# Rotary table and key norm column as one array, loaded inside the branch on the score bound (Perceiver layer, one core)

## The chip, the cores and the metric

The kernel runs on one core of one Trainium2 chip. The metric is the device time of one execution in microseconds, and a kernel's figure is the median of its runs. Profiles are of one execution each. In what follows PE is TensorE's matmul, PEld its weight loads, DVE is VectorE, ACT is ScalarE, POOL is GpSimd, and SP is the sync engine, which only asks for transfers here; "ACTq" and "SPq" are the queues from which ScalarE and SP ask for DMAs. L104 is line 104 of the kernel before.

## The reference

One layer over 256 tokens of width 512, in three residual parts: cross attention, a state-space (Mamba-2) block, and a mixture of 32 experts with 6 per token and one shared expert. Only the first part touches the change:

```python
q = rms_norm((x @ wq).reshape(B, L, 16, 128), q_norm_w)
k = rms_norm((x @ wk).reshape(B, L, 4, 128), k_norm_w)
v = (x @ wv).reshape(B, L, 4, 128)
k_ctx = rms_norm((h_ctx_kv @ wk_ctx).reshape(B, T, 4, 128), k_norm_w)     # T = 4096
v_ctx = (h_ctx_kv @ wv_ctx).reshape(B, T, 4, 128)
cos, sin = rope_cache(L, 128, 10000.0, x.dtype)
q = q * cos + rotate_half(q) * sin
k = k * cos + rotate_half(k) * sin
k_full = concatenate([k_ctx, k]); v_full = concatenate([v_ctx, v])        # repeated for 4 heads each
out = softmax(q @ k_full * scale + mask) @ v_full @ wo                    # the 256 own keys are causal
...
x = x + xattn(layernorm(x), ctx); x = x + mamba(layernorm(x)); x = x + moe(layernorm(x))
```

All of it is fp32. `x` is normalised before it is projected, so the queries and own keys need the layer norm, while the 4096 context keys and values need only `ctx_2048`, `wk_ctx` and `wv_ctx`.

## The kernel before, in words

The program has a short common part and then a branch. The common part (L78 to L138) loads the two norm weights into one row, `nw` (L87), and computes from them a bound on the attention scores (L107 to L110). Every engine loads the resulting flag (L1599) and goes into one of two arms, each of which is a full layer; with these inputs it is the arm `layer(lctx, True)`, `bounded`, which subtracts a constant in the softmax instead of a running maximum. Ahead of the flag SP also asks for what the first matmuls need, in this order:

- the first context slice, `ctx0[:, 0]`, 256 KB (L97, recorded as L94);
- the context key weights, the `wkc` half of the tile `wkv`, in three pieces of 256, 256 and 512 KB (L98 to L100, recorded as L95);
- `x_sb`, the tokens, 512 KB (L101);
- the second slice of `ctx0`, 256 KB, and the last two, 512 KB (L102, L103);
- the context value weights `wvc`, 1024 KB (L104).

ScalarE asks for `nw`, and then for three tables: `rope` (cosine and sine of 256 positions by 64 frequencies, 128 KB, L133), `w_bc` (the two norm weights broadcast to all 128 partitions, 128 KB, L135), and `kw_col` (the key norm weight as a column, one word per partition, L138).

Inside the arm SP goes on with the projection weights: `wk`, `wq0`, `wv`, `wq1` to `wq3` of 1024 KB each (`wpiece`, L189), then the next pieces of the context (`load_ctx`, L240). The matmuls of the start run in this order on TensorE: three key pieces of the first context block (`key_piece`, tile `ps_k`, four products over k with one of the four `wkc` slices each; in fp32 a product shows as two rows), eight transposes of the normalised `x` (`turn_xn`, tile `lnT`), the first value piece (`ps_v`, which needs `wvc`), and the self blocks (`ps_self`, with `wk` and `wq`), between which the other pieces of the first context block stand. After that come the attention over nine blocks of keys and values, the state-space part and the experts.

The tables are used by VectorE and ScalarE. `rope_table` (L436) multiplies the cosines and sines by the norm weights, in eight operations, L441 and L442, into a part of `oacc`; `norm_rope` (L446) uses the result when the first self block is done. `bounded_attention` takes two maxima over `w_bc` (L555, L556). `kw_col` scales the queries at L630. On VectorE the layer norm (`bn_stats` L201, then L203, L195, and `xn` at L206) stands in the same in-order queue as L441 and L442. In the program of before, the order there is: both `bn_stats`, one `bn_aggr`, L441, and then the operations of the two groups in turn.

The framework writes each engine's order from its own estimates of the times, except where the code pins it (`keep_in_program_order`, `issue_after`). It also gives the completion of DMAs from SP and ScalarE to eight semaphores in turn: a DMA first waits for the one that had the same semaphore before it, eight places earlier in the common order of both queues. In the program of before, that order begins: `nw`, `ctx0` slice 0, `rope`, `wkc` piece 0, `w_bc`, `kw_col`, `wkc` piece 1, `wkc` piece 2, `x_sb`, `ctx0` slice 1, `ctx0` slices 2 and 3, `wvc`, and, in the arm, `wk`, `wq0`, `wv`, `wq1`. So slice 1 of `ctx0` waits for slice 0, slices 2 and 3 for `rope`, `wvc` for `wkc` piece 0, `wk` for `w_bc`, and `wq0` for `kw_col`.

Of the kernel before, what the change touches and what calls it, by code (L numbers as in the profile page):

```python
# [11 lines left out]
FP = mybir.dt.float32  # L12
# [7 lines left out]
P = 128  # L20
L = 256
NT = L // P
# [9 lines left out]
HALF = HD // 2  # L32
# [34 lines left out]
def rope_tables():  # L67
    inv = (1.0 / np.float32(THETA) ** (np.arange(0, HD, 2, dtype=np.float32) / np.float32(HD))).astype(np.float32)
    freqs = np.outer(np.arange(L, dtype=np.float32), inv).astype(np.float32)
    return np.stack([np.cos(freqs), np.sin(freqs)], axis=1).astype(np.float32)  # L70
# [3 lines left out]
def perceiver_layer(ctx: ExitStack, tc: tile.TileContext, a: dict, out: bass.AP):  # L74
    nc = tc.nc
    V, S, G, TE = nc.vector, nc.scalar, nc.gpsimd, nc.tensor

    early = ctx.enter_context(tc.tile_pool(name="early", bufs=1))  # L78
    const = ctx.enter_context(tc.tile_pool(name="const", bufs=1))
# [49 lines left out]
    blocks_d = [tc.dram_tile((REP, HD, P), FP, name=f"qd{i}") for i in range(NT * NH // REP)]  # L129
    sums_d = [tc.dram_tile((SH, P), FP, name=f"sums{t}") for t in range(NT)]  # L130

    rope = const.tile([P, NT, 2, HALF], FP, name="rope")
    S.dma_start(rope, a["rope"].rearrange("(t p) c h -> p t c h", p=P))  # L133
    w_bc = const.tile([P, 2, HD], FP, name="w_bc")
    S.dma_start(w_bc, a["norm_ws"].partition_broadcast(P))  # L135
    qw_bc, kw_bc = w_bc[:, 0, :], w_bc[:, 1, :]
    kw_col = const.tile([P, 1], FP, name="kw_col")
    S.dma_start(kw_col, a["norm_ws"][1, :].unsqueeze(1))  # L138

    def layer(ctx, bounded):  # L140
        small = ctx.enter_context(tc.tile_pool(name="small", bufs=4))
        wpool = ctx.enter_context(tc.tile_pool(name="wpool", bufs=6))
        kvp = ctx.enter_context(tc.tile_pool(name="kvp", bufs=2))
# [1456 lines left out]
    with tc.If(flag == 1) as arms:  # L1600
        with ExitStack() as lctx:
            layer(lctx, True)
    with arms.Else():
        with ExitStack() as lctx:
            layer(lctx, False)


def expert_weights(wg, wu, wd):

    c = np.ascontiguousarray  # L1610
    gu = np.concatenate([wg, wu], axis=2).reshape(NE, KD, P, 2 * FE).transpose(0, 2, 1, 3).reshape(NE, P, WGU)
    return {"experts": c(np.concatenate([gu, wd[:, 0:P]], axis=2)), "down_rest": c(wd[:, P:])}


def host_layout(i):

    c = np.ascontiguousarray
    f = {k: np.asarray(v) for k, v in i.items()}
    xa, ma, fa = "L0_xattn_", "L0_attn_", "L0_ffn_"
    d = {  # L1620
        "x": c(f["x"][0]),
        "ctxT": c(f["ctx_2048"][0].reshape(NC, CK // P, P, KD, P).transpose(0, 4, 1, 3, 2)),
        "rope": rope_tables(),
        "W_inT": c(f[ma + "W_in"].T),
        "W_outT": c(f[ma + "W_out"].T),
        "by_channel": c(np.concatenate([f[ma + "conv_w"].reshape(XCT, P, CONV).transpose(1, 0, 2).reshape(P, XCT * CONV),
                                        f[ma + "conv_b"].reshape(XCT, P).T, f[ma + "norm_weight"].reshape(DIT, P).T],
                                       axis=1)),
        "by_head": c(np.stack([f[ma + k] for k in ("dt_bias", "A_log", "D")])),
        "sgu": c(np.stack([f[fa + "sg"], f[fa + "su"]], axis=1)),  # L1630
        **expert_weights(f[fa + "wg"], f[fa + "wu"], f[fa + "wd"]),
    }
    d.update({k: c(f[xa + k]) for k in ("wq", "wk", "wv", "wo", "wk_ctx", "wv_ctx")})
    d["norm_ws"] = c(np.stack([f[xa + "q_norm_w"], f[xa + "k_norm_w"]]))
    d.update({k: c(f[fa + k]) for k in ("gate_w", "sd")})
    return d
# [15 lines left out]
```

## Time and profile before

| | |
|---|---|
| median of 3 runs | 985.41 us (983.65 to 986.29) |
| profiled execution, own time | 989.13 us |
| its span, first to last instruction | 987.4 us |
| instructions | 8877 |
| PE busy | 964.3 us (98%) |
| DVE, ACT, POOL busy | 496.5, 388.1, 205.0 us |
| moved by DMA | 125.65 MB, mean 127 GB/s |
| ScalarE's HWDGE queue (q10) | 4178 packets, 5.85 MB |
| SP's queue (q1) | 119216 packets, 77.96 MB |

A timeline row gives start, length, engine, line, operation, and in brackets how long the engine had been idle before and what ended that. A row with "x3" merges three instructions. A row of the waits gives who waited for what, the sum in us, how often, and the longest. A row of the windows gives the stretch, the busy time of PE, PEld, DVE, ACT and POOL in it with the number of instructions, the granted TensorE clock, the busy share of the DMA engines, and GB/s. The ends of matmul rows are modelled, so that TensorE's own pace is better seen from the starts of its weight loads.

### The profile page before, as it was taken

Reading aid. Unit: us, or ns where it says so; the run is one execution under the profiler, and the core shown is the slowest. Engines: PE = TensorE matmul, PEld = TensorE weight load, DVE = VectorE, ACT = ScalarE, POOL = GpSimd, SP = SyncE. Lnnn points to the kernel's source line nnn. Section 1 sums busy time; section 2 is a strip of 40 time slices with the busy share of each in tenths; the row PEclk is TensorE's granted clock in tenths of the full one; section 3 lists DMA queues with packets and bytes.
Section 4 is the critical chain, followed back from the end, with each engine's and each line's share of the span. In section 5 each row is a group of like instructions: output and inputs, shape, how many; then the busy total and the mean of one; then the engine's idle time right before and its main releaser. Section 6 shows DMA issues by size and latency. Waiting matters only on the chain.

```text
span 987.4 us, 8877 instructions
## 1 busy us (share of the span) xinstructions
PE 964.3 (98%) x2730; PEld 453.8 (46%) x2730; DVE 496.5 (50%) x1000; ACT 388.1 (39%) x854; POOL 205.0 (21%) x212
## 2 busy tenths in 40 slices
PE   7999999999999999999999999999999999999995
PEld 3444444444444444444444444444465655455442
DVE  3456554454454544544545445458587666521133
ACT  3645443443444434434434344344153731122220
POOL 4443001101100200200200110000013234545442
PEclk9999999999999999999999999999999999999999
DMA  9733232213304304304113121250046452899973
GB/s 317 237 74 98 76 95 91 71 32 117 85 11 139 85 1 149 75 11 150 53 33 97 67 51 32 72 152 1 0 150 206 171 188 111 319 342 352 381 292 107
DMA packets 131436, 125.65 MB, mean 127 GB/s; under 512 B 80209, under 2 KB 99570, under 8 KB 126130
## 3 DMA queue, kind: packets, MB, share of 16 engines
q1 hardware_dynamic: 119216, 77.96, 26.1%
q0 software_dynamic: 7984, 41.16, 11.4%
q10 hardware_dynamic: 4178, 5.85, 1.6%
q8 instruction: 24, 0.39, 0.2%
q14 instruction: 34, 0.28, 0.1%
HBM read 89.02 MB, written 35.93 MB: 127 GB/s over the span
## 4 chain that ended last, share of the span: by engine, by line
PE 94%; DVE 2%; ACT 1%; POOL 1%; issue 1%; DMA 1%; SPq 0%; DVEq 0%; ACTq 0%
PE oT L592 23%; PE scT L567 23%; PE ps_kv L364 17%; PE ps_egu L218 5%; PE ps_self L218 3%; PE ps_v L218 2%; PE ps_o L790 2%; PE ps_egu L1388 2%; PE ps_k L218 2%; PE ps_ye L1458 2%; PE ps_xbc L218 1%; PE ps_out L984 1%; PE ps_sgu L218 1%; PE xgTp L1369 1%; PE ps_ye L1461 1%; PE ps_yd L924 1%
## 5 line engine op out<-in xcount | busy, mean ns | idle before, releaser
L583 DVE TENSOR_TENSOR lacc<-lacc,prT 128x512 f32<-128x512 f32 x256 | 182.8, 715 | 238.9 <-ACT prT L573 238.2
L573 ACT ACTIVATE prT<-scT,bq,rk 128x512 f32<-128x512 f32 x256 | 198.9, 777 | 253.8 <-PE scT L567 241.7
L567 PE MATMUL scT<-qT,kT 128*128 128x512 f32 x536 | 271.6, 592 | 0.0
L592 PE MATMUL oT<-prT,v 128*128 128x512 f32 x528 | 268.3, 592 | 0.0
L567 PEld LDWEIGHTS scT<-qT,kT 128*128 128x128 f32 x536 | 101.1, 190 | 124.7 <-issue 122.4
L592 PEld LDWEIGHTS oT<-prT,v 128*128 128x128 f32 x528 | 100.2, 190 | 125.8 <-issue 115.5
L196 POOL TENSOR_TENSOR rk<-pv,mhalf 128x4 f32<-128x4 f32 x32 | 32.3, 1010 | 369.2 <-DVE pv L195 369.2
L364 PE MATMUL ps_kv<-wkv,fast 128*128 128x512 f32 x112 | 53.4, 592 | 0.0
L254 ACT ACTIVATE sq<-kraw 128x128 f32<-128x128 f32 x128 | 35.6, 278 | 45.3 <-DVE kraw L382 43.2
L364 PE MATMUL ps_kv<-wkv,ctx 128*128 128x512 f32 x112 | 52.8, 592 | 0.0
L364 PE MATMUL ps_kv<-fast,fast 128*128 128x512 f32 x112 | 52.6, 592 | 0.0
L598 DVE TENSOR_TENSOR oacc<-oT,oacc 128x512 f32<-128x512 f32 x64 | 43.7, 683 | 0.0
L364 PEld LDWEIGHTS ps_kv<-wkv,fast 128*128 128x128 f32 x112 | 21.3, 190 | 26.8 <-issue 26.8
L364 PEld LDWEIGHTS ps_kv<-fast,fast 128*128 128x128 f32 x112 | 21.3, 190 | 26.8 <-issue 21.8
L364 PEld LDWEIGHTS ps_kv<-wkv,ctx 128*128 128x128 f32 x112 | 21.3, 190 | 26.8 <-issue 23.7
L358 POOL TENSOR_TENSOR fast<-ctx 128x512 f32<-128x512 f32 x7 | 9.3, 1335 | 113.0 <-PE ps_kv L364 94.2
L382 DVE TENSOR_TENSOR kraw<-ps_kv,fast 128x256 f32<-128x256 f32 x42 | 17.9, 426 | 28.1 <-PE ps_kv L364 28.1
L1441 DVE TENSOR_TENSOR hid<-si,ps_egu 128x128 f32<-128x128 f32 x18 | 5.2, 287 | 51.7 <-ACT si L1439 49.0
L790 PE MATMUL ps_o<-wo,qT 128*128 128x512 f32 x64 | 28.8, 592 | 0.0
L218 PE MATMUL ps_self<-wq,xT 128*128 128x512 f32 x64 | 28.1, 592 | 0.0
L603 DVE RECIPROCAL lacc<-ps_l 128x512 f32<-128x512 f32 x8 | 26.8, 3349 | 0.1
L364 PE MATMUL ps_kv<-fast,ctx 128*128 128x512 f32 x56 | 26.3, 592 | 0.0
(379 smaller groups left out, 1120.8 us busy)
## 6 DMA issues: line engine op xcount, KB each, us to landing
xg<-xn SPq DMA_DIRECT2D x6, 2560.0 KB
ctx<-in_ctxT_dram SPq DMA_DIRECT2D x7, 1024.0 KB, 5.3
kd<-tr SPq DMA_DIRECT2D x112, 64.0 KB, 2.7
kT<-kd SPq DMA_DIRECT2D x28, 256.0 KB, 3.7
ye<-y_sb ACTq DMA_DIRECT2D x21, 256.0 KB, 7.9
wq<-in_wq_dram SPq DMA_DIRECT2D x4, 1024.0 KB
wo<-in_wo_dram SPq DMA_DIRECT2D x4, 1024.0 KB
w_in<-in_W_inT_dram SPq DMA_DIRECT2D x4, 1024.0 KB
```

The costliest lines, as they stand in the source:

```text
L196: return G.tensor_tensor(dst, v[:, :n], mhalf[:, :n], ALU.pow)
L218: TE.matmul(ps, lhs(k), rhs_of(k), start=(k == 0), stop=(k == KD - 1))
L254: S.activation(sq[:, h, :], raw[:, h, :], AF.Square, accum_out=ss[:, h:h + 1])
L364: TE.matmul(ps, lhs(k), rhs(k), start=(start and k == 0), stop=(k == 1), skip_group_check=True)
L567: scored.append(TE.matmul(sc, kT[:, g, i * P:(i + 1) * P], qT[:, t, heads4(g), :].rearrange("p h q -> p (h q)"), start=True, stop=True).ins)
L573: S.activation(pr, sc, AF.Exp, bias=shift, scale=SCALE if r is None else r[:, i, g:g + 1])
L583: V.tensor_tensor(la, la, pr, ALU.add)
L592: TE.matmul(outs[g, t], v[:, i, g * HD:(g + 1) * HD], pr, start=(n == 0), stop=last)
L598: V.tensor_tensor(ov, outs.pop((g, t)), ov, ALU.add)
L603: V.reciprocal(rl, ps)
L790: TE.matmul(m["ps_o", t], aT[:, t, h, :], wo[j][:, h % 4, :], start=(h == 0), stop=(h == NH - 1))
L1388: TE.matmul(ps[self.half(i)], xT[:, k, self.half(i)], w[i][:, k, :], start=(k == 0), stop=(k == KD - 1))
```

## The change

The host builds one array, `tables`, of 128 partitions by 257 words: for a partition p, the cosines and sines of the positions p and 128 + p, and the p-th key norm weight as the last word. The tile `tables` takes the place of the tiles `rope` and `kw_col`, which become views of it. The tile `w_bc` stays as it is. The two loads that are left, `tables` and `w_bc`, stand at the head of `layer`, that is inside each arm, behind the branch; the DMA that filled `kw_col` is gone. The number of operations on other engines does not change.

```diff
-    rope = const.tile([P, NT, 2, HALF], FP, name="rope")
-    S.dma_start(rope, a["rope"].rearrange("(t p) c h -> p t c h", p=P))
+
+    tables = const.tile([P, NT * 2 * HALF + 1], FP, name="tables")
+    rope = tables[:, 0:NT * 2 * HALF].rearrange("p (t c h) -> p t c h", t=NT, c=2)
+    kw_col = tables[:, NT * 2 * HALF:]
     w_bc = const.tile([P, 2, HD], FP, name="w_bc")
-    S.dma_start(w_bc, a["norm_ws"].partition_broadcast(P))
     qw_bc, kw_bc = w_bc[:, 0, :], w_bc[:, 1, :]
-    kw_col = const.tile([P, 1], FP, name="kw_col")
-    S.dma_start(kw_col, a["norm_ws"][1, :].unsqueeze(1))
 
     def layer(ctx, bounded):
+
+        S.dma_start(tables, a["tables"])
+        S.dma_start(w_bc, a["norm_ws"].partition_broadcast(P))
         small = ctx.enter_context(tc.tile_pool(name="small", bufs=4))
...
-        "rope": rope_tables(),
+        "tables": c(np.concatenate([rope_tables().reshape(NT, P, 2 * HALF).transpose(1, 0, 2).reshape(P, NT * 2 * HALF),
+                                    f[xa + "k_norm_w"].reshape(P, 1)], axis=1)),
```

## The prediction

> **What bounds the kernel now.** I read the chain of work first. Over the whole span it lies on TensorE (94%), so a change at the start counts only if it moves the moment from which TensorE runs without a gap. Its first pieces, cut at 80 us:
>
> ```profile
> PE 94%; DVE 2%; ACT 1%; POOL 1%; issue 1%; DMA 1%; SPq 0%; DVEq 0%; ACTq 0%
> ...
> 1.73 6.33 DMA wkv<-in_wk_ctx_dram
> 8.06 0.04 issue
> 8.11 12.28 PE ps_k L218 x22
> 20.39 0.87 PE lnT L212 x8
> ```
>
> The reader sees a load of the context key weights that ends at 8.06, then TensorE up to the end. Everything that the change touches lies ahead of 20 us, and what matters is when the three key pieces (ps_k, 24 rows: 3 pieces x 4 products x 2 passes) are over: at 20.22, where the first turn of the normalised x starts. Second, the weight loads in the timeline, since the ends of matmul rows are modelled:
>
> ```profile
> 5.48 0.50 PEld L218 LDWEIGHTS ps_k<-wkv,ctx 128*128 128x128 f32 x2 [5.48 <-issue]
> 8.11 0.50 PEld L218 LDWEIGHTS ps_k<-wkv,ctx 128*128 128x128 f32 x2 [2.12 <-DMA wkv<-in_wk_ctx_dram]
> 9.94 0.50 PEld L218 LDWEIGHTS ps_k<-wkv,ctx 128*128 128x128 f32 x2 [1.33 <-DMA wkv<-in_wk_ctx_dram]
> ...
> 11.81 0.34 PEld L218 LDWEIGHTS ps_k<-wkv,ctx 128*128 128x128 f32 x1 [0.52 <-issue]
> 12.66 0.34 PEld L218 LDWEIGHTS ps_k<-wkv,ctx 128*128 128x128 f32 x1 [0.52 <-issue]
> 13.36 0.19 PEld L218 LDWEIGHTS ps_k<-wkv,ctx 128*128 128x128 f32 x1 [0.36 <-issue]
> 13.79 0.19 PEld L218 LDWEIGHTS ps_k<-wkv,ctx 128*128 128x128 f32 x1 [0.24 <-issue]
> ```
>
> Each of the first three products waits for its own slice of wkv (ready at 5.5, 8.1, 9.9). Passes are 0.85 us apart (11.81 to 12.66) until about 13.2, and 0.43 (13.36 to 13.79) from there on: so late loads cost twice, once as a gap and once as a late start of the fast pace. The granted clock reads 1.00 all along and doesn't show this.
>
> Third, who shares the DMA engines then. ScalarE's queue asks for the tables at 1.37 to 2.77, and SP's own queue waits for them:
>
> ```profile
> 1.37 0.41 ACTq L133 DMA_DIRECT2D rope<-in_rope_dram  x1
> 1.82 0.48 ACTq L135 DMA_DIRECT2D w_bc<-in_norm_ws_dram  x1
> 2.32 0.45 ACTq L138 DMA_DIRECT2D kw_col<-in_norm_ws_dram  x1
> ...
> SPq L94 <- DMA ctx<-in_ctxT_dram: 1.6, 1, 1.6
> SPq L189 <- DMA kw_col<-in_norm_ws_dram: 1.1, 1, 1.1
> ...
> SPq L94 <- DMA rope<-in_rope_dram: 0.6, 1, 0.6
> SPq L189 <- DMA w_bc<-in_norm_ws_dram: 0.6, 1, 0.6
> ...
> 4.00:4.50 0.50, 0.00 (x0) 0.00 (x0) 0.00 (x0) 0.00 (x0) 0.00 (x0) 1.00 1.03 358
> ...
> 7.50:8.00 0.50, 0.06 (x1) 0.00 (x0) 0.00 (x0) 0.00 (x0) 0.00 (x0) 1.00 0.76 232
> ...
> 9.50:10.00 0.50, 0.50 (x2) 0.06 (x1) 0.00 (x0) 0.00 (x0) 0.00 (x0) 1.00 1.09 422
> ```
>
> The last two columns of the windows are DMA share and GB/s. The waits name the landings: rope near 5.7, w_bc near 8.2, kw_col near 9.7 (wq0 issued at 9.75). While they are under way the engines move 203 to 291 GB/s (5.5 to 9.0), afterwards about 400. The tables are first used on VectorE at 12.56 (L441), kw_col at 83.5 (L630).
>
> **The change part by part.** Its own sum is made against the profiled execution, 989.13 (span 987.4 and 1.73 around it). That run lies 3.7 over the median of the runs shown, 985.41, so I carry the difference over as a share.
>
> 1. Taken from the time ahead of the flag: three DMAs of ScalarE, 0.41 + 0.48 + 0.45 of issue on a queue that next has compute at 13.61: worth nothing by itself. Their transfers are 128 + 128 + 0.5 KB. What SP needs for the first product is 512 KB (first context slice, first weight slice). From 1.5 to 5.5 the windows add up to 844 KB, so up to some 250 KB may have been ScalarE's and instruction code. At the 265 to 358 GB/s seen there, rope alone is 0.4 to 0.5 us and both some 0.9. So the first product starts 0.4 to 1.3 earlier by this. Bound from below: the flag load on TensorE ends at 2.9 + 0.49 = 3.4, and SP, whose load ends at 7.27, was ready for its first DMA behind the branch at 8.24 - 0.6 = 7.64, so 0.37 more: 3.8. From above: 5.5, no gain, if code and not data held it. I take 4.5.
>
> 2. The second slice: landed 2.6 after the first one, with w_bc beside it. Alone, 256 KB at 300 to 400 GB/s is 0.7 to 0.9: near 5.4, while the first product ends at 4.5 + 2.05 = 6.55. This gap (7.56 to 8.11) goes. The third slice, 512 KB: 1.3 to 1.7 more, near 7.1, and with the moved tables beside it up to 1 later; needed at 6.55 + 1.83 = 8.4. No gap either.
>
> 3. Pace. Before, the fast pace came at about 13.2, 5.1 after the last clear gap ended at 8.11. With the same 5.1 from 4.5 it comes at 9.6: by then 2 passes (to 6.55) and 3.05 / 0.855 = 3.6 more are done; 18.4 are left at 0.4286 = 7.9. End 17.5 against 20.22: gain 2.7. If the count runs from 9.94 instead (3.3 us of unbroken work), the fast pace comes at 7.8, 3.5 passes done, 20.5 x 0.4286 = 8.8, end 16.6: gain 3.6. The Trainium skill (TensorE: Matmul & The Clock Gate, Part 1) says that the full clock is granted after one busy window of about 3.4 us, and that windows run freely, so the wait is 3.4 to 6.8 after work begins. The switch at 13.2 fits that from 8.11, not cleanly from 9.94 (3.3). By the rule it falls between 7.9 and 11.3, so end 16.7 to 18.3, gain 1.9 to 3.5, middle 2.7: I keep 2.7, and the rule gives the spread, which a repeated run can show too.
>
> 4. Added behind the branch: two DMAs on ScalarE, 257 and 256 words a partition. They are not free to go at once: SP and ScalarE take eight completion semaphores in turn, so each waits for the DMA eight places back, here the first context slice and one of the first weight slices: issue at about 4 to 5.5. ScalarE has nothing queued behind them until the table load at 13.61, so that wait holds no one. In flight they took 4.2 to 6.4 us before; 4.2 to 6.4 from 4 to 5.5 is 8 to 12. One transfer less, and the slow tail of 4-byte pieces (kw_col, 1.5 us behind w_bc) is gone. The skill's DMA: Bandwidth & Descriptors, Rules for kernel authors, speaks against the move: a DMA should be issued early and waited for late. By the rule the tables lose 3 us of lead, and VectorE would stand in rope_table up to that long if it had no slack. The row says first use at 12.56, behind bn_stats, which itself waits for x_sb until 11.28. I take a stall of nothing; both ends 0 and +1 on VectorE, covered by the slack of part 6.
>
> 5. SP: its waits on rope (0.6), w_bc (0.6) and kw_col (1.1) go, as does the 1.6 on the first context slice (this now takes a fresh semaphore). The second and third context loads go out at 3.2 to 4.1 instead of 4.76 to 6.1, wvc by 4.7 instead of 6.15, wk by about 6 instead of 8.24. Since the engines are full from 9 on, bytes and not issue decide then; wvc, which landed at 15.9 (POOL's first weight sum waits for it), comes about 1 earlier and is needed at 18.4; wk (18.5 before) is needed near 22.2.
>
> 6. What is late next: the second context slice, needed when piece 0 ends, near 10.7. It comes behind 2.36 MB of SP's and ScalarE's bytes, which the windows reach at 10.7 before; at 350 to 400 GB/s from 2.5 it lands at 9.5 to 10.5. Cost 0 to 1; I take 0.1. Then xn: it was ready at 14.9, 3.6 after x_sb's landing, and is needed at 17.5 instead of 20.22, so slack falls from 5.3 to 2.6 or more. POOL issues no part of this; its sums move with wvc.
>
> Sum: 2.7 less 0.1 = 2.6 us; 985.41 x (1 - 2.6 / 989.13) = 982.8.
>
> **The rivals.**
>
> *A, as above.* For: the three waits on wkv are in the rows. With the start between 3.8 and 5.0 and the window's spread, gain 1.5 to 4.0: 981.4 to 983.9, and with repeats 0.5 wider.
>
> *B, the contention is only pushed along.* The tables meet the third weight slice and the second context slice instead; TensorE starts at 5.0 but waits near 8.5 and again near 10, and the fast pace comes 4 after that. End near 19.2 to 19.7: gain 0.5 to 1, 984.7. For: the 256 KB still have to pass before 12. Against: 1.3 MB of SP's bytes are ahead of them by then. The case in which instruction code holds the first product ends here too.
>
> *C, the tables come too late.* VectorE works in order; if L441 stays ahead of the xn of L206 in its queue, xn follows the tables' landing by 12.56 to 14.89, 2.3 us. TensorE stands at lnT from a landing of 15.2 on, and the kernel gets slower than before from 17.9 on, one for one: a landing at 21 (16 us of flight, behind wvc, wk and wq0 in the shared engines) costs 3 us, 988.4. Against: 6.4 us is the longest flight seen. The nearest relative has the same sign: the scheduler that writes the arm's order sees other times of arrival, and puts instructions in another order on PE, worth a few us either way.
>
> *D, it doesn't do what it says*: it does, as the tables' DMAs stand in the layer's arm; but if the scheduler puts them behind SP's wk and wq0 in the turn of the semaphores, they wait for the third slice (near 7), which leads to B or C.
>
> **How the numbers follow.** 0.3% of the time, about what a measurement of this kernel can tell from no change, is 2.96 us: below 982.45 is faster, above 988.4 slower. A 0.65, B 0.16 (with D), C with a changed order 0.19. A's middle lies 0.4 short of the bound, but its spread reaches 1.4 above it and 1.1 below, and a start at 3.8 (gain 3.3) is about as near to the evidence as one at 4.5: 0.38 of its 0.65 goes to the far side, the rest to no change. B is no change; C is slower by 1 to 5: 0.18 beyond the bound, 0.01 within. Faster 0.38, same 0.44, slower 0.18. Range: 980.0 leaves out the best 0.06 of A, 987.3 some 0.14 of C. A's and B's own range is 980.5 to 985.2.
>
> **What would show it.** Right: no wait of SP on rope, w_bc or kw_col; the first three pairs of ps_k weight loads 2 us apart or less from a start before 5; the pace 0.43 by 11.3; lnT at 16.5 to 18.3; afterwards the same rows, shifted. Wrong: the first pair still at 5.4, or pairs two and three released by DMA wkv; L441 waiting for tables beyond 13; or a changed order of matmuls behind 20 us, with gaps that have nothing to do with the start.

## The result and the profile after

| | before | after |
|---|---|---|
| median, 16 runs each | 984.64 us (983.44 to 986.30) | 983.02 us (981.86 to 984.89) |
| ratio, with its 95% interval | | 0.9983 (0.9976 to 0.9990) |
| profiled execution, own time | 989.13 us | 983.11 us |
| its span | 987.4 us | 981.4 us |
| start of the `lnT` transposes | 20.2 us | 18.1 us |
| first weight load of `ps_self` | 24.86 us | 22.71 us |

The changed kernel is 1.6 us faster (1.0 to 2.4 by the interval). That is a real gain, and smaller than the 0.3% that the prediction called a difference. The two profiles differ by far more, 6.0 us, and this must not be read as the gain. The profiled execution of before, 989.13, lies above the slowest of its 16 runs, 986.30. Stage by stage, the rows of after run 2.1 to 2.2 us ahead of those of before from `lnT` to the start of the experts (845.0 before, 842.9 after). Another 3.4 us appear between the first product of the experts (`ps_egu`) and the last product of the kernel (`total`), where the change touches nothing. That stretch took 132.0 us in the profile of before and 128.6 here; in the profiles of the experiments it took 128.6 to 129.0 on one chip and 131.2 to 133.5 on two others, whatever the kernel. The medians of before differ by chip in the same way (985.3, 989.5 and 990.8), so every ratio below is taken against runs of before on the same chip.

In the code after, lines lie two further down: the key pieces are L220, `lnT` L214, `xn` L208, and the table operations L443 and L444.

First the chain of waits of after, in order of time (start and length in us, what):

```profile
1.26 3.85 DMA wkv<-in_wk_ctx_dram
5.10 0.14 issue
5.24 13.00 PE ps_k L220 x24
18.24 0.87 PE lnT L214 x8
```

The chain now has one transfer and then 13 us of key products in one piece. The first weight slice lands at 5.10. The timeline of the weight loads shows the same from TensorE's side:

```profile
5.21 0.50 PEld L220 LDWEIGHTS ps_k<-wkv,ctx 128*128 128x128 f32 x2 [5.21 <-issue]
6.22 0.34 PEld L220 LDWEIGHTS ps_k<-wkv,ctx 128*128 128x128 f32 x1 [0.52 <-DMA wkv<-in_wk_ctx_dram]
7.08 0.34 PEld L220 LDWEIGHTS ps_k<-wkv,ctx 128*128 128x128 f32 x1 [0.52 <-issue]
...
9.64 0.34 PEld L220 LDWEIGHTS ps_k<-wkv,ctx 128*128 128x128 f32 x1 [0.52 <-issue]
10.35 0.19 PEld L220 LDWEIGHTS ps_k<-wkv,ctx 128*128 128x128 f32 x1 [0.38 <-issue]
10.78 0.19 PEld L220 LDWEIGHTS ps_k<-wkv,ctx 128*128 128x128 f32 x1 [0.24 <-issue]
...
18.08 0.80 PEld L214 LDWEIGHTS lnT<-ident,xn 128*128 128x128 f32 x7 [0.29 <-issue]
```

The first pair starts at 5.21. The next loads follow at the plain slow pace, 0.86 us apart (6.22 to 7.08), with an idle time of 0.52 that belongs to that pace: the gaps before the second and third slice are gone. From the row of 10.35 on, a load takes 0.19 and the next one follows after 0.43. This short row is the mark of the fast pace that I use below; here it comes 5.1 us after the first load. Next, the queues of ScalarE and SP (timeline, then SP's waits), and VectorE's timeline:

```profile
4.24 0.37 ACTq L141 DMA_DIRECT2D tables<-in_tables_dram  x1
5.75 0.34 ACTq L142 DMA_DIRECT2D w_bc<-in_norm_ws_dram  x1
...
SPq L191 <- DMA wkv<-in_wk_ctx_dram: 1.9, 1, 1.9
...
SPq L191 <- DMA x_sb<-in_x_dram: 0.7, 1, 0.7
...
9.33 1.29 DVE L203 BATCH_NORM_STATS2 bn<-x_sb 128x6 f32<-128x512 f32 x2 [6.46 <-DMA x_sb<-in_x_dram]
11.65 1.16 DVE L208 TENSOR_SCALAR xn<-x_sb,mv,rs 128x512 f32<-128x512 f32 x2 [0.63 <-POOL rs L198]
14.43 0.29 DVE L443 TENSOR_TENSOR oacc<-tables,w_bc 128x128 f32<-128x128 f32 x1 [1.62 <-DMA w_bc<-in_norm_ws_dram]
```

SP waits for no table any more. `x_sb` is there at 9.3 instead of 11.3. And one thing is new in the program: both `xn` (11.65) stand ahead of all the table operations in VectorE's queue, where before they stood behind five of the eight. PE, POOL and SP have the same order as before, and so has ScalarE apart from the moved loads. `w_bc` is the late one: asked for at 5.75, it holds VectorE until 14.4. Last, windows of 0.5 us (the last two columns are the busy share of the DMA engines and GB/s):

```profile
7.50:8.00 0.50, 0.50 (x2) 0.04 (x1) 0.00 (x0) 0.00 (x0) 0.00 (x0) 1.00 0.99 379
...
10.50:11.00 0.50, 0.50 (x3) 0.23 (x2) 0.50 (x5) 0.00 (x0) 0.00 (x0) 1.00 1.02 188
11.00:11.50 0.50, 0.50 (x2) 0.19 (x1) 0.02 (x1) 0.04 (x1) 0.46 (x1) 1.00 0.94 123
```

At 7.5 to 8.0 the engines move 379 GB/s where before they moved 232. The slow stretch has not vanished, though: at 10.5 to 11.5 they are busy all the time and move 123 to 188 GB/s. It has gone to a place where TensorE waits for nothing.

### The profile page after: what moved, and what is told of

Same layout as the page of the kernel before. It is cut to its first block, busy times and chain, and to the rows that moved or that the text cites. A ratio compares the mean times of both kernels' runs of the same rounds, so it can differ in the third digit from the quotient of the medians.

```text
span 981.4 us, 8877 instructions
## 1 busy us (share of the span) xinstructions
PE 961.9 (98%) x2730; PEld 454.0 (46%) x2730; DVE 497.0 (51%) x1000; ACT 388.0 (40%) x854; POOL 204.5 (21%) x212
## 3 DMA queue, kind: packets, MB, share of 16 engines
q0 software_dynamic: 7984, 41.16, 11.3%
## 4 chain that ended last, share of the span: by engine, by line
PE 95%; ACT 1%; DVE 1%; POOL 1%; issue 0%; DMA 0%; SPq 0%; DVEq 0%
PE oT L594 23%; PE scT L569 23%; PE ps_kv L366 17%; PE ps_egu L220 5%; PE ps_self L220 3%; PE ps_v L220 2%; PE ps_o L792 2%; PE ps_egu L1390 2%; PE ps_k L220 2%; PE ps_ye L1460 2%; PE ps_xbc L220 1%; PE ps_out L986 1%; PE ps_sgu L220 1%; PE xgTp L1371 1%; PE ps_ye L1463 1%; PE ps_ye L1413 1%
## 5 line engine op out<-in xcount | busy, mean ns | idle before, releaser
L366 PEld LDWEIGHTS ps_kv<-wkv,ctx 128*128 128x128 f32 x112 | 21.3, 190 | 26.8 <-issue 23.7
L220 PE MATMUL ps_self<-wq,xT 128*128 128x512 f32 x64 | 28.1, 592 | 0.0
```

The source lines that it names most:

```text
L220: TE.matmul(ps, lhs(k), rhs_of(k), start=(k == 0), stop=(k == KD - 1))
L366: TE.matmul(ps, lhs(k), rhs(k), start=(start and k == 0), stop=(k == 1), skip_group_check=True)
```

## The experiments

The theory was the prediction's: the place of the loads decides, because they share the engines with the slices that the first products need, and every late slice costs a gap and a late start of the fast pace. Rivals were that the merging does it, that contention is only pushed along, and that later tables hold VectorE and through it TensorE.

### Place or merging: e1_move_only and e2_merge_only

The first takes the kernel before and moves its three loads as they are to the head of `layer`; the second takes the changed kernel and asks for its two loads ahead of the branch.

```diff
 # e1_move_only, from the kernel before
-    S.dma_start(rope, ...)
-    S.dma_start(w_bc, ...)
-    S.dma_start(kw_col, ...)
     def layer(ctx, bounded):
+        S.dma_start(rope, ...)
+        S.dma_start(w_bc, ...)
+        S.dma_start(kw_col, ...)
 # e2_merge_only, from the kernel after
+    S.dma_start(tables, a["tables"])
+    S.dma_start(w_bc, a["norm_ws"].partition_broadcast(P))
     def layer(ctx, bounded):
-        S.dma_start(tables, a["tables"])
-        S.dma_start(w_bc, a["norm_ws"].partition_broadcast(P))
```

> The three old transfers (rope, w_bc, kw_col, each as it was) asked for behind the branch; no merged array. Theory (the place decides: what shares the DMA engines before wkv's slices have landed): as the changed kernel, ratio 0.9983 to before within 0.001, lnT starts near 18.1, the three pairs of ps_k weight loads unbroken from 5.2. Rival (the merge decides, by doing away with 512-byte rows and the 4-byte column): gain under 0.5 us, lnT past 19.5. Late column: kw_col may land up to 2 us after w_bc, used only at 81 us, so no cost.

> The merged array tables and w_bc, both asked for ahead of the flag as before; no move. Theory (place): most of the gap stays, since 256 KB still share the engines with the weight slices: first product near 5.5, second slice at 7 to 8, lnT 19 to 20.2, gain 0 to 1 us. Rival (merge): gap gone, lnT near 18.1, gain 1.6 us.

Measured: 0.9994 (0.9985 to 1.0004) for the move alone, 1.0009 (0.9999 to 1.0019) for the merging alone. The weight loads, of e1_move_only and then of e2_merge_only:

```profile
5.06 0.50 PEld L218 LDWEIGHTS ps_k<-wkv,ctx 128*128 128x128 f32 x2 [5.06 <-issue]
...
11.17 0.19 PEld L218 LDWEIGHTS ps_k<-wkv,ctx 128*128 128x128 f32 x1 [0.49 <-issue]
```

```profile
5.49 0.50 PEld L220 LDWEIGHTS ps_k<-wkv,ctx 128*128 128x128 f32 x2 [5.49 <-issue]
8.12 0.50 PEld L220 LDWEIGHTS ps_k<-wkv,ctx 128*128 128x128 f32 x2 [2.13 <-DMA wkv<-in_wk_ctx_dram]
9.43 0.29 PEld L220 LDWEIGHTS ps_k<-wkv,ctx 128*128 128x128 f32 x1 [0.81 <-DMA wkv<-in_wk_ctx_dram]
```

With the loads behind the branch the products run unbroken; with them ahead, merged or not, the second slice is waited for (2.13 here), as before the change. So the place is what removes the gaps, and merging two of three loads does not. VectorE's order, too, goes with the place: `xn` ahead of the tables in e1_move_only, behind in e2_merge_only. In time, the move alone can't be told from no change, nor clearly from the whole change, whose interval (0.9976 to 0.9990) overlaps its own; its fast pace came late in the profile (11.17), and `lnT` started at 18.5. That the place brings the 1.6 us of time is thus not shown by this pair: it is argued from the rows of the start.

### Which table is it: e8_column_ahead, e9_w_bc_ahead, e4_one_array

Three kernels, each run once and all on one chip, each made from the kernel after: a 4-byte column loaded ahead of the branch in addition; `w_bc` alone ahead of the branch; and no broadcast load at all, the host having laid the 128 copies of the two norm weights beside the tables, so that one plain transfer of 257 KB stands behind the branch.

```diff
 # e8_column_ahead
+    column = const.tile([P, 1], FP, name="column")
+    S.dma_start(column, a["norm_ws"][1, :].unsqueeze(1))
 # e9_w_bc_ahead
+    S.dma_start(w_bc, a["norm_ws"].partition_broadcast(P))
     def layer(ctx, bounded):
         S.dma_start(tables, a["tables"])
-        S.dma_start(w_bc, a["norm_ws"].partition_broadcast(P))
 # e4_one_array
-    w_bc = const.tile([P, 2, HD], FP, name="w_bc")
+    w_bc = tables[:, NT * 2 * HALF + 1:].rearrange("p (i d) -> p i d", i=2)
...
-        S.dma_start(w_bc, a["norm_ws"].partition_broadcast(P))
```

> The changed kernel with a column load like the old kw_col (128 pieces of 4 bytes, not used) alone ahead of the flag. If small pieces hold the engines out of proportion to their bytes: first or second weight slice 0.5 us or more later than 5.2 and 6.2. If bytes decide: no difference over 0.2 us.

> The changed kernel with w_bc alone asked for ahead of the flag again; the merged tables stay behind the branch. One look at the landings. If w_bc (128 copies of one row, 128 KB) is what held the second weight slice: its weight load at 7 to 8 instead of 6.1, a gap behind the first product. If rope or the sum of bytes did it: within 0.4 us of the changed kernel's 6.16 to 6.22, and the first product some 0.2 later than 5.2.

> The broadcast weights are laid out by the host as further columns of tables: one transfer of 257 KB behind the branch in place of two, no row read 128 times. If the broadcast read is why w_bc was 8.7 us under way and why the windows from 10.5 to 11.5 moved 123 to 188 GB/s at a full share: one landing before 11, no such dip, first table operation right behind xn (near 12.8). If the ring's turn decides: landing past 13 as before. TensorE's start the same in both (5.2, unbroken).

Of e9_w_bc_ahead, the first weight load and two windows:

```profile
6.58 0.50 PEld L220 LDWEIGHTS ps_k<-wkv,ctx 128*128 128x128 f32 x2 [6.58 <-issue]
...
4.00:5.00 1.00, 0.00 (x0) 0.00 (x0) 0.00 (x0) 0.00 (x0) 0.00 (x0) 1.00 0.87 142
5.00:6.00 1.00, 0.00 (x0) 0.00 (x0) 0.00 (x0) 0.00 (x0) 0.00 (x0) 1.00 0.80 97
```

The window of e8_column_ahead from 4 to 5:

```profile
4.00:5.00 1.00, 0.00 (x0) 0.00 (x0) 0.00 (x0) 0.00 (x0) 0.00 (x0) 1.00 0.46 136
```

Then the two windows in which the changed kernel has its slow stretch, first of the changed kernel and then of e4_one_array:

```profile
10.00:11.00 1.00, 1.00 (x3) 0.38 (x2) 1.00 (x6) 0.00 (x0) 0.00 (x0) 1.00 1.05 284
11.00:12.00 1.00, 1.00 (x3) 0.38 (x2) 0.37 (x2) 0.54 (x1) 0.96 (x2) 1.00 0.97 196
```

```profile
10.00:11.00 1.00, 1.00 (x4) 0.44 (x3) 0.88 (x5) 0.02 (x1) 0.10 (x1) 1.00 1.03 400
11.00:12.00 1.00, 1.00 (x3) 0.38 (x2) 0.49 (x1) 1.00 (x1) 1.00 (x2) 1.00 1.05 408
```

With `w_bc` alone ahead of the branch the start is late in this one profile, though in another form than in the kernel before: the engines are 80 to 87% busy and move 97 to 142 GB/s, the first product starts at 6.58 instead of 5.21 (5.55 in e4_one_array, on the same chip), and then nothing is waited for. I had expected the second slice to be late, not the first. What the column costs is not settled. The engines are half idle in the window above, but the first product, at 5.74, comes half a microsecond behind the changed kernel's 5.21 and only 0.2 behind e4_one_array's 5.55. And without the broadcast read there is no slow stretch: e4_one_array moves 400 to 408 GB/s where the changed kernel moves 284 and 196, and its first table operation runs at 12.59, right behind `xn`, without a wait.

So the slow stretch goes with the read of one 1 KB row for 128 partitions, not with the 128 KB that it delivers. But that read is not enough to bring it about. In e3_late, shown below, the same load is asked for at 12.56 and has landed at 18.1, and in all of that time the engines move 378 to 387 GB/s. Two of its windows:

```profile
15.00:16.00 1.00, 1.00 (x4) 0.41 (x3) 0.63 (x1) 0.94 (x5) 1.00 (x1) 1.00 1.06 378
16.00:17.00 1.00, 1.00 (x4) 0.49 (x3) 0.50 (x1) 0.94 (x6) 0.92 (x2) 1.00 1.05 379
```

The rows there are as small as in the changed kernel, so the size of the pieces alone doesn't do it either. What must come together with the read stays open. The three single times (987.65, 990.78, 988.49, with before at 990.82, from 988.43 to 993.03) can't be told apart well, and I read only the profiles.

### Too late: e3_late and e5_sp_last

Rival C put to the test in two ways: e3_late has ScalarE ask for both tables behind the first copy of a key piece, e5_sp_last has SP ask for them behind `wvc`, still ahead of the branch.

```diff
 # e3_late: in the layer's order of work, in place of the head of layer
+        with tc.issue_after(key_copies[0]):
+            S.dma_start(tables, a["tables"])
+            S.dma_start(w_bc, a["norm_ws"].partition_broadcast(P))
 # e5_sp_last: ahead of layer, in place of its head
+    nc.sync.dma_start(tables, a["tables"])
+    nc.sync.dma_start(w_bc, a["norm_ws"].partition_broadcast(P))
```

> Tables and w_bc asked for by ScalarE behind its first key copy, near 13.5. Tests the price of lateness (the case in which the tables hold VectorE). Theory: front as in the changed kernel to lnT (18.1), but w_bc lands at 20 to 23, and on VectorE the table operations stand ahead of the copies of xT, which are then done 2.5 us after the landing: ps_self, which starts at 23.0 in the changed kernel, starts at 23 to 26, so 0 to 3 us more than the changed kernel, one for one. Rival (transfers hidden anyway, lateness is free): ps_self at 23.0, and as fast as the changed kernel.

> Tables (merged) and w_bc asked for by SP, ahead of the flag, behind wvc: nothing moved behind the branch, but nothing of them ahead of the weight slices either. Theory (what counts is that they don't share the engines with wkv, and not the branch): first products unbroken from 5.2 as in the changed kernel. But they wait for wvc's turn in SP's ring and land near 15 to 16, and the program puts L443 ahead of xn on VectorE: xn near 17.5 to 18.5, so TensorE may wait up to 1 us at lnT. Ratio 0.998 to 0.9995. Rival (the branch itself matters): first product back at 5.5 and gaps of 0.5 and more.

Measured: e5_sp_last 1.0034 (1.0021 to 1.0047), slower than before; e3_late 1.0004 (0.9995 to 1.0013), no gain left. In both the key products start at 5.15 and 5.28, wait less than 0.2 us for data, and are fast from 8.7, among the best starts without a warm-up, so the loss is behind it. In e5_sp_last the loads stand ahead of the branch, and the start is clear all the same: what clears it is not the branch but that the loads are asked for behind the urgent slices. VectorE's and POOL's timelines in e5_sp_last, and what TensorE waited for:

```profile
15.23 0.29 DVE L443 TENSOR_TENSOR oacc<-tables,w_bc 128x128 f32<-128x128 f32 x1 [4.69 <-DMA w_bc<-in_norm_ws_dram]
...
17.81 2.63 DVE L208 TENSOR_SCALAR xn<-x_sb,mv,rs 128x512 f32<-128x512 f32 x1 [0.45 <-POOL rs L198]
20.36 2.49 DVE L443 TENSOR_TENSOR oacc<-tables,w_bc 128x128 f32<-128x128 f32 x1
...
17.75 2.41 POOL L332 TENSOR_TENSOR oacc<-wkv 128x1024 f32<-128x1024 f32 x1
20.23 2.47 POOL L333 TENSOR_TENSOR oacc<-wkv,oacc 128x1024 f32<-128x1024 f32 x1
...
PE lnT L214 <- DVE xn L208: 2.6, 1, 2.6
PE ps_self L220 <- DVE xT L215: 2.3, 1, 2.3
```

The loads stand ahead of the branch, and so the scheduler again puts a table operation ahead of `xn`: VectorE is held 4.69 us for `w_bc`. The delay then runs into POOL's three sums over `wvc`. Operations that take 0.28 (L443) and 0.55 (`xn`) alone take 2.49 and 2.63 beside them, ending as POOL's does. The Trainium skill (SBUF — State Buffer, SBUF: two separate sides) says that VectorE and GpSimd share a pair of ports under an exclusive lock, which VectorE needs for operations with two inputs from SBUF, as L443 has, or in a mode that uses both ports, and that the later of the two stands for the whole instruction; the pairs of rows agree, each VectorE row ending within 0.3 us of the POOL row it started in. A copy whose input lies in PSUM, where TensorE writes its products, is not held: in the changed kernel the two `xT` copies, at 19.14, take 1.27 together while POOL's sum of 19.21 runs to 21.60. Whether `xn`, which has one large input, is in such a mode no run shows. TensorE pays twice, 2.6 at `lnT` and 2.3 at `ps_self`, whose first load comes at 27.28.

In e3_late `xn` is early (11.75), as in the changed kernel, but the tables land at 18.1, and `xT`, the copy that the self blocks wait for, is queued behind the table operations, one of which again takes 2.50 beside POOL. Its VectorE and PEld rows:

```profile
18.13 0.98 DVE L443 TENSOR_TENSOR oacc<-tables,w_bc 128x128 f32<-128x128 f32 x1 [1.63 <-DMA w_bc<-in_norm_ws_dram]
...
23.55 1.28 DVE L213 COPY xT<-lnT 128x512 f32<-128x512 f32 x2
...
24.29 0.30 PEld L218 LDWEIGHTS ps_self<-wk,xT 128*128 128x128 f32 x2 [2.36 <-DVE xT L213]
...
27.53 0.34 PEld L218 LDWEIGHTS ps_self<-wk,xT 128*128 128x128 f32 x1 [0.52 <-issue]
28.38 0.34 PEld L218 LDWEIGHTS ps_self<-wk,xT 128*128 128x128 f32 x1 [0.52 <-issue]
29.10 0.19 PEld L218 LDWEIGHTS ps_self<-wk,xT 128*128 128x128 f32 x1 [0.38 <-issue]
```

Here the wait costs twice. After it the weight loads are 0.85 apart again, and the fast pace is back only at 29.10; from the start of `ps_self` to that of the experts this profile takes 821.9 us, the changed kernel's 820.1. In e5_sp_last, after gaps of 2.84 and 2.50, the pace stays fast.

So rival C exists, with two doors: `xn` behind the tables, and `xT` behind them. The changed kernel passes both, with its tables at 14.4.

### The pace: e6_warm, e7_warm_before, e10_warm_ctx_first, e11_after_again

If the fast pace comes some time after TensorE begins to work, nine products of a constant with itself, into a PSUM tile that nobody reads, while the first slices are still on their way, should bring it forward. e6_warm adds them to the changed kernel, e7_warm_before to the kernel before. e10_warm_ctx_first is e6_warm with the second context slice asked for ahead of `x_sb`. e7b_warm_before is e7_warm_before again, on another chip. e11_after_again is the changed kernel once more, beside the others on their chip.

```diff
 # e6_warm, e7_warm_before, e10_warm_ctx_first
     G.memset(ones, 1.0)
+    with tc.tile_pool(name="warm", bufs=1, space=PSUM) as warm:
+        ps_warm = warm.tile([P, P], FP, name="ps_warm")
+        for i in range(9):
+            TE.matmul(ps_warm, ones, ones, start=(i == 0), stop=(i == 9 - 1))
 # e10_warm_ctx_first, too
-    nc.sync.dma_start(x_sb, ...)
     load_ctx0(1, 1)
+    nc.sync.dma_start(x_sb, ...)
```

> The changed kernel with nine extra 128x128 matmuls of a constant tile on TensorE ahead of the flag, from about 1.3 us on; their result is not used. Theory (half of the gain was an earlier start of the fast pace, which comes by TensorE's activity and not by the data): fast pace between 4.7 and 8.1 instead of 10.2, lnT near 17, 1.0 us (0.5 to 1.5) less than the changed kernel, some 2.6 less than before (ratio 0.9974). Rival (the data alone decide the pace of the products): no change to the changed kernel, lnT 18.1.

> The kernel before with the same nine extra matmuls ahead of the flag. Theory: the gaps stay (weight loads at 5.5, 8.1, 9.9, by the data), but the pace is fast by 9.9, so 20 passes of 0.43 follow: lnT near 18.5, gain 1.5 us (ratio 0.9985), about what the change gives by another way. Rival (only the gaps count, the pace follows data): lnT 20.2, no gain. If the gap of 2 us takes the fast pace away again: in between.

> The kernel before with the nine extra matmuls once more, since its trace showed lnT 1.9 us earlier and its time no gain. Theory (a front's gain holds, the earlier pair fell badly): 0.5 to 2 us less than before (ratio 0.998 to 0.9995), lnT 18.3 to 19.5. Rival (the fast pace is lost again in the gaps of 1.4 and 2.0 us in many executions, and the profiled one was a lucky one): lnT between 18.3 and 20.2 in this profile, ratio 0.999 to 1.0005.

> The changed kernel with the nine extra matmuls ahead of the flag, and the second slice of ctx0 asked for ahead of x_sb. In the kernel with the extra matmuls alone the second key piece waited 1.1 us for that slice (9.68). Theory: the wait goes, x_sb lands some 0.7 later (9.5), xn is ready near 12.5 and isn't yet needed; lnT at 15.7 instead of 16.7; 4.5 us less than before, ratio 0.9955. Rival (xn becomes the last, or the third piece waits for slices 2 and 3): lnT 16.7 or later, ratio as with the extra matmuls alone, 0.9965.

> The changed kernel once more, beside the others of this call. Theory (the front sets the gain, and it holds to the end): 1.6 us less than before (ratio 0.9983, within 0.001), lnT between 17.3 and 18.9 as the free clock window falls. Rival (on some chips the experts' stage, where DMA shares are highest, gives the gain back, as the move alone suggested with 0.9994): ratio over 0.999 with lnT still near 18.

Measured: e6_warm 0.9965 (0.9951 to 0.9979), e10_warm_ctx_first 0.9965 (0.9954 to 0.9976), e11_after_again 0.9981 (0.9974 to 0.9988), e7_warm_before 1.0004 (0.9995 to 1.0014) and, on another chip, 1.0001 (0.9990 to 1.0012). The weight loads of e6_warm:

```profile
1.20 3.92 PEld L119 LDWEIGHTS ps_warm<-ones 128*128 128x128 f32 x18 [1.20 <-POOL ones L115]
5.06 0.50 PEld L224 LDWEIGHTS ps_k<-wkv,ctx 128*128 128x128 f32 x2
...
6.66 0.19 PEld L224 LDWEIGHTS ps_k<-wkv,ctx 128*128 128x128 f32 x1 [0.24 <-issue]
...
9.68 0.30 PEld L224 LDWEIGHTS ps_k<-wkv,ctx 128*128 128x128 f32 x2 [1.11 <-DMA ctx<-in_ctxT_dram]
```

The fast pace comes at 6.66, and `lnT` at 16.7, though faster products now outrun the second context slice (1.11). Asking for that slice earlier only moves the wait, as this row of e10_warm_ctx_first shows, and the time stays:

```profile
8.10 0.30 PEld L224 LDWEIGHTS ps_k<-wkv,ctx 128*128 128x128 f32 x2 [1.19 <-DMA wkv<-in_wk_ctx_dram]
```

The time at which the fast pace begins is not fixed. The first row of 0.19 came this long after TensorE's unbroken work began:

| profile | work begins | first short row | after |
|---|---|---|---|
| after | 5.21 | 10.35 | 5.1 |
| e11_after_again, the same kernel | 5.14 | 8.61 | 3.5 |
| e5_sp_last / e3_late / e4_one_array | 5.15 / 5.28 / 5.55 | 8.71 / 8.67 / 9.01 | 3.6 / 3.4 / 3.5 |
| e1_move_only / e9_w_bc_ahead | 5.06 / 6.58 | 11.17 / 12.41 | 6.1 / 5.8 |
| e6_warm | 1.20 | 6.66 | 5.5 |
| e2_merge_only, from its last clear gap | 8.12 | 12.23 | 4.1 |

All lie between 3.4 and 6.1. The prediction's estimate from the rule that it weighed, a window that runs freely, is 3.4 to 6.8. The rule would explain why two profiles of the same kernel differ by 1.7 us here, with `lnT` at 18.1 in one and 17.2 in the other; the window itself is seen in no run.

With the warm-up the kernel before gains nothing, although both of its profiles have `lnT` at 18.3 and 18.5, nearly 2 us ahead of the profile of before. Its rows show where a faster pace goes when data is late (e7_warm_before):

```profile
7.08 0.30 PEld L222 LDWEIGHTS ps_k<-wkv,ctx 128*128 128x128 f32 x2 [1.39 <-DMA wkv<-in_wk_ctx_dram]
9.39 0.30 PEld L222 LDWEIGHTS ps_k<-wkv,ctx 128*128 128x128 f32 x2 [2.01 <-DMA wkv<-in_wk_ctx_dram]
...
11.35 0.30 PEld L222 LDWEIGHTS ps_k<-wkv,ctx 128*128 128x128 f32 x2 [0.81 <-DMA ctx<-in_ctxT_dram]
```

Waits of 1.39, 2.01 and 0.81 stand where the slow products were. That explains why the gain is small, not the 2 us between the profiles. A likely reading is that the one profile of before was a late one. Against the first load of `ps_self` in each profile, the times line up:

| profile | first `ps_self` load | ratio | ratio less 1, of 985 us |
|---|---|---|---|
| e6_warm | 21.29 | 0.9965 | -3.4 |
| e10_warm_ctx_first | 21.42 | 0.9965 | -3.4 |
| e11_after_again | 21.83 | 0.9981 | -1.9 |
| after | 22.71 | 0.9983 | -1.7 |
| e7_warm_before, two chips | 22.96, 23.12 | 1.0004, 1.0001 | +0.4, +0.1 |
| e1_move_only | 23.10 | 0.9994 | -0.6 |
| e2_merge_only | 24.17 | 1.0009 | +0.9 |
| e3_late | 24.29 | 1.0004 | +0.4 |
| e5_sp_last | 27.28 | 1.0034 | +3.4 |

A straight line through these ten has a slope of 1.1 us of time per us of start, with the points up to 1.3 off it, and it meets a ratio of 1 at 23.7. The profile of before has 24.86. So what the start gains does reach the end, about one for one, and a usual run of before would start its self blocks about 1 us earlier than the profiled one. This is worked out from the line and not shown, since the kernel before was profiled only once.

The best kernel is the changed one with the warm-up: beside each other on one chip, e10_warm_ctx_first has a median of 981.81 us and the changed kernel 983.07.

## Why the prediction was right, point by point

The time said was 982.8, measured 983.02; a gain of 2.6 was said and 1.6 measured. That the times agree to 0.2 us is in part luck: the base of the sum, 985.41 from three runs, came out as 984.64 over 16. The likeliest case, A, is what happened; the terms of its sum were these.

1. **The start** was the term that was mis-sized. It was taken at 4.5 out of 3.8 to 5.5, and came at 5.24 on PE, its weight load at 5.21 (5.06 to 5.55 in the kernels without a warm-up in which ScalarE asks for no table ahead of the branch), so a start before 5, named as a sign of being right, did not come. Without tables the engines still move only 47 to 225 GB/s from 1.5 to 3.5, and SP's own transfers behind the first slice share them. So clearing ScalarE's bytes away helped the later slices and hardly the first: against the weight load at 5.48 before, 0.3 of the gain is here, and not the 1.0 that was counted.
2. **The gaps** before the second and third slice are gone, as said. e1_move_only and e2_merge_only show that the place does it.
3. **The pace** came 5.1 after the start, as said, and from the later start this gives `lnT` at 18.1, inside the 16.5 to 18.3 expected, and a gain of 2.1 between the two profiles instead of 2.7. The rule's spread was more than a margin: it is what one profile differs from the next by.
4. **The two loads behind the branch** were issued at 4.24 and 5.75, as said, but flew 6.8 and 8.6 us by the trace's list of DMA issues, not 4.2 to 6.4; `w_bc` landed at 14.4, beyond the 8 to 12 expected and beyond the mark of 13 under "wrong". The 6.4 that the prediction took for the longest flight left out `kw_col`, which by its own reading was 7.4 under way (2.32 to 9.7). Without the broadcast read (e4_one_array) the tables are there by 12.59; why that read is slow here and not in e3_late, where it flies 5.5, stays open. That no stall reached TensorE was right, and partly for another reason than the one given: not the old order with its slack, but a new order with `xn` ahead of the tables. In the old order, `xn` would have ended 2.3 behind the landing, an estimate of 16.8 with the prediction's own figure in rival C, still ahead of 18.1. The rule that the prediction took from the Trainium skill (DMA: Bandwidth & Descriptors, Rules for kernel authors), to issue a DMA early, was followed too little in e3_late and too much before the change: of all that was measured, right behind the branch is the best place.
5. **SP's waits** on the tables and the 1.6 on the context slice are gone, as said. SP waits 1.9 and 0.7 for other loads, which holds nothing that is needed soon; `wk` went out at 5.62 (said: about 6). `wvc` came no earlier for it: POOL's first sum, which waits for it, starts at 16.71 against 15.92 before, 0.8 later where 1 earlier was said. It is needed at 18.84, so this costs nothing.
6. **What is late next**: the second context slice costs nothing visible in after and 0.05 in e11_after_again (an idle time of 0.29 where 0.24 is usual); 0.1 was said. It is the next wait as soon as products are faster: 1.11 in e6_warm.

Rival B had the start nearer (5.0) and was wrong in its consequence: contention is pushed along, but to 10.5 to 11.5, where no slice is waited for. Rival C did not happen; its price was set too low. It put the point of no stall at a landing of 15.2 and the break-even at 17.9. In e5_sp_last a landing of 15.2 already costs more than the whole gain, because the delayed operations meet POOL's sums and take 2.5 us each, which no step of the prediction had. In e3_late a landing of 18.1 costs the gain too, by `xT` and not by the `xn` that the rival named. The changed order of the scheduler, feared there as a harm, came on VectorE alone and did good.

## What to carry to other kernels

When the first products of a kernel wait for data, look at who else is in the DMA engines then: a small table that is first used 10 us later costs what it delays, so ask for it once the urgent transfers have been issued, but well before its first use, and see on the consumer's in-order queue what stands behind it. Measure early gains several times, since the pace switch alone moves the front of one and the same kernel by about a microsecond. And give TensorE idle-time work while it waits for its first operand only if the operand then keeps up: the same nine products were worth about 1.3 us where the data was early (e10_warm_ctx_first against the changed kernel) and nothing where it was late.

## What the runs showed of the hardware that I had not expected

- While one 1 KB row was read for 128 partitions, the DMA engines moved only 97 to 196 GB/s at a share of 0.80 or more (e9_w_bc_ahead, after); the same values laid out in 128 rows passed at 400 to 408 (e4_one_array). In e3_late the same broadcast read passed at 378 to 387.
- A column of 128 words, 512 bytes, put ahead of the first slices went with a DMA share of 0.46 from 4 to 5 us, where e4_one_array has 1.04. Its price at the start, 0.2 to 0.5 us, is not settled.
- A 128x128 multiplication on VectorE takes 0.28 us alone and 2.49 beside one of POOL's 128x1024 operations of 2.4 us, while a copy from PSUM beside such an operation is not held.
- The fast pace can be lost again: in e3_late after a wait of 2.36 us, for 3.5 us; in e5_sp_last, after 2.84 and 2.50, it was not.
- The granted clock reads 1.00 while products run at half pace; the spacing of the weight loads shows the pace, and it changes 3.4 to 6.1 us after work begins.
